# Reordering the steps of a neighbourhood-attention layer: earlier queries, projections and transposes behind the scores, bias tables spread over the opening

## The chip, the cores and the metric

The kernel runs on one core of a Trainium2 chip, in one launch. The metric is the device time of that launch in microseconds (us). Five engines of a core work side by side, each through its own instructions in order: PE (TensorE: matmuls and transposes, its weight loads listed as PEld), ACT (ScalarE), DVE (VectorE), POOL (GpSimd) and SP (SyncE, which here only issues DMAs). They wait for each other by semaphores.

## What is computed

Four layers over an image batch x of 4 x 56 x 56 x 128, all in fp32. The change concerns layer 0 alone, a neighbourhood attention with 4 heads of 32 channels, in which each pixel looks at the 7 x 7 pixels around it:

```python
qkv = (x @ w_qkv + b_qkv).reshape(B_, H_, W_, 3, nh, hd)
...
k_win = kk[:, :, idx_i][:, :, :, :, idx_j]
v_win = v[:, :, idx_i][:, :, :, :, idx_j]
...
attn = jnp.einsum('bnijd,bnipjqd->bnijpq', q, k_win) + bias[None]
attn = jax.nn.softmax(attn.reshape(B_, nh, H_, W_, k * k), axis=-1)
...
out = jnp.einsum('bnijpq,bnipjqd->bnijd', attn, v_win)
...
x = x + _L0_conv_ref(_gn(x), L0_conv_w_qkv, L0_conv_b_qkv, L0_conv_rpb, L0_conv_w_proj, L0_conv_b_proj)
```

`_gn` is a group norm over each image and group of 4 channels, and the last step of the layer is `out @ w_proj + b_proj`. Layer 1 is a selective scan, layer 2 a tanh attention and a mixture of experts, layer 3 an attention and a mixture of experts; their code is the same before and after.

## The kernel before

**Tiles.** The four images lie in SBUF for the whole program, as X[b]. In layer 0 (`layer0`, L354) an image is cut into NCH = 7 chunks of SEQ = 8 pixel rows, CH = 448 pixels. A chunk's keys are taken in bands of 8 columns; a band's window of 14 rows x 8 columns fills 112 partitions. The 7 bands are done in two groups, the even ones (four bands) and the odd ones (three), so a chunk gives two **units** and the four images give 28 chunks and 56 units. Even unit numbers are the groups of four.

**Steps.** For each chunk: `queries` (L438: one matmul group, then ACT writes q), `keys` (L447: the same into the one key buffer kT), `values` (L459: in two halves, each copied out by ACT). For each unit: `scores` (L481: PE writes two psum tiles "s" of two banks each), `weights` (L495: ACT takes exponentials, then DVE multiplies three heads and POOL one by a table of exponentiated biases), `sums` (L508: PE sums weights times values into psum "o", and the weights alone into "d"). After a chunk's second unit, `finish` (L526) has four steps: `copied` (L532: ACT copies d and o out of psum, POOL adds the projection's bias to X), `divided` twice (L539: DVE takes reciprocals of half the denominators and multiplies), `projected` (L544: PE multiplies by w_proj, DVE adds the result to X at L550).

**The next image's norm** runs beside an image. `norm_steps` (L401) has twelve steps: seven `chunk` steps, each with four transposes of X on PE (`turn`, L225), their statistics on DVE (`stats`, L235) and a copy of the raw transposes by ACT (`raw_bands`, L219); then the aggregate, two small matmuls that average over a group, with DVE steps after them and a square root on ACT; then the root with the normalisation of four chunks on DVE, and `hand_over` with the other three. In the last image `next_norm` (L424) does the same for layer 1, without the raw copies.

**Buffers.** Queries, keys, each half of the values, transposes, projections and the group matmuls all write to the psum tag "m", which has two buffers: each of these waits until the user of the buffer two allocations before is through. The tag "s" has two buffers, "o" and "d" one each; q, v and oT have two in SBUF.

**Order.** The program fixes the order on PE, ACT, DVE and POOL by hand (`manual_schedule`, L369); only waits are added. Before the loop come the bias tables: `bias_tables` (L301) loads its inputs, `spread` lays them out, and each of 24 `table` steps (L339) has four matmuls into an "s" buffer and one exponential on ACT. Eight are made at once, one after each of the seven chunk steps of the first image's norm, four during its group matmuls, five in the loop's first iteration. Image 0 is loaded from ACT's queue in four cuts ahead of the tables' inputs; all other loads come from SP's queue.

The loop (L601) is a plan: the dictionary `mid` holds steps that an iteration issues before its sums, `at` those that it issues after them:

```python
for i in range(len(units) + 5):
    if i + 1 < len(units):
        scores(i + 1)
        weights(i + 1)
    for step in mid.get(i, []):
        step()
    if 0 <= i - 1 < len(units):
        sums(i - 1)
    for step in at.get(i, []):
        step()
```

So iteration i issues the scores and weights of unit i+1 and the sums of unit i-1. `first[k]` is the first unit of chunk k (2k). The queries of chunk k+1 stand in `at` of iteration first[k], right before the iteration that issues their first scores. The keys of a chunk stand in `at` at a place given by its number, the values and the chunk steps of the norm in `mid`, the other norm steps and the four steps of `finish` in `at`. Some 50 small steps that prepare layer 1's weights (`next_weights`, L597; most on DVE) are spread over `at` too.

Of the kernel before, what the change touches and what calls it, by code (L numbers as in the profile page):

```python
# [18 lines left out]
B, HW, C = 4, 56, 128  # L19
# [3 lines left out]
NT = S // TP  # L23
TC = 4
CH = TC * TP
NCH = S // CH
SEQ = CH // HW
# [111 lines left out]
class Hybrid:  # L139
# [214 lines left out]
    def layer0(self, wp1):  # L354
# [3 lines left out]
        nc, a, tc = self.nc, self.a, self.tc  # L358
        ET = mybir.EngineType
        with ExitStack() as ctx:  # L360
# [6 lines left out]
            m = lambda: self.t(ps_m, [P, 512], "m")  # L367
            ctx.enter_context(
                tc.manual_schedule(engines={ET.PE, ET.Activation, ET.DVE, ET.Pool})  # L369
            )  # L370
            self.load_image(0, nc.scalar, (0, TC, 3 * TC, 5 * TC, NT))
            tables, spread, table = self.bias_tables(
                wp, wp, lambda: self.t(sm, [TP, NH, CH], "e", bufs=3).rearrange("p h n -> p (h n)"), m,
                lambda: self.t(ps_s, [P, 2, 512], "s")[:TP, 0],
            )
            group = self.load(wp, [P, P], "group", a["k_group"])
            wqkv = self.load(wp, [P, 3 * C], "wqkv", a["L0_conv_w_qkv"])
            bqkv = self.t(wp, [P, 3], "bqkv")
# [15 lines left out]
            chunks = [(b, c) for b in range(B) for c in range(NCH)]  # L394
            units = [(k, g) for k in range(len(chunks)) for g in range(len(PARTS))]
# [5 lines left out]
            def norm_steps(b):  # L401
                g = self.group_norm(b, big, group)

                def chunk(c):
                    if c == 0:
                        g.place_bands(big)
                    g.turn(c, m)
                    g.stats(c)
                    g.raw_bands(c)

                def hand_over():
                    g.normed(range(4, NCH))
                    xn[b] = g.xn

                parts = g.groups(m)
                both = lambda fs: lambda: [f() for f in fs]
                return (
                    [lambda c=c: chunk(c) for c in range(NCH)]
                    + [parts[0], both(parts[1:3]), both(parts[3:5])]
                    + [lambda: (parts[5](), g.normed(range(0, 4))), hand_over]  # L420
                )


            def next_norm():  # L424
                g = self.first_norm = self.group_norm(0, wp1, group)
                parts = g.groups(m)
                both = lambda fs: lambda: [f() for f in fs]
                chunk = lambda c: lambda: (g.turn(c, m), g.stats(c))
                return (
                    [chunk(c) for c in range(NCH)]  # L430
                    + [parts[0], both(parts[1:3]), both(parts[3:5]), parts[5]]
                )
# [40 lines left out]
            def parts(i):  # L473

                got, at = [], 0
                for band, j0, j1 in PARTS[units[i][1]]:
                    got.append((band, j0, j1, at))
                    at += j1 - j0
                return got

            def scores(i):  # L481
                k, g = units[i]
                t = top(chunks[k][1])
                sc[i] = [self.t(ps_s, [P, 2, 512], "s") for _ in range(2)]
                for band, j0, j1, at in parts(i):
                    for h in range(NH):
                        own = slice(h * HD, (h + 1) * HD)
                        to = sc[i][h // 2][:TP, h % 2, : SEQ * WIDTHS[g]]
                        nc.tensor.matmul(
                            by_row(to, WIDTHS[g])[:, :, at : at + j1 - j0],  # L490
                            kT[own, band, t : t + ROWS, :].rearrange("p r j -> p (r j)"),
                            by_row(q[k][own, :])[:, :, j0:j1], start=True, stop=True,
                        )

            def weights(i):  # L495
                k, g = units[i]
                c = chunks[k][1]
                n = SEQ * WIDTHS[g]
                es[i] = e = self.t(sm, [TP, NH, CH], "e", bufs=3)
                for j, s in enumerate(sc.pop(i)):  # L500
                    nc.scalar.activation(e[:, 2 * j : 2 * j + 2, :n], s[:TP, :, :n], AF.Exp)
                tab = tables[0 if c == 0 else 2 if c == NCH - 1 else 1]
                at = sum(WIDTHS[:g])
                for eng, h0, h1 in ((nc.vector, 0, 3), (nc.gpsimd, 3, NH)):
                    p = e[:, h0:h1, :n].rearrange("p h (q j) -> p h q j", j=WIDTHS[g])
                    eng.tensor_tensor(p, p, tab[:, h0:h1, :, at : at + WIDTHS[g]], op=ALU.mult)
# [19 lines left out]
            def finish(k):  # L526

                b, c = chunks[k]
                x = self.X[b][:, TC * c : TC * (c + 1), :]
                r = {}  # L530

                def copied():  # L532
                    r["o"], r["d"] = self.t(sm, [P, CH], "oT"), self.t(sm, [P, CH], "d", bufs=1)
                    ps = dict(zip("od", out.pop(k)))
                    for n in "do":
                        nc.scalar.copy(r[n], ps[n][:, :CH])
                    nc.gpsimd.tensor_add(x, x, bproj.unsqueeze(1).to_broadcast([TP, TC, C]))

                def divided(n):  # L539
                    own = slice(n * 2 * TP, (n + 1) * 2 * TP)  # L540
                    nc.vector.reciprocal(r["d"][:, own], r["d"][:, own])
                    nc.vector.tensor_mul(r["o"][:, own], r["o"][:, own], r["d"][:, own])

                def projected():  # L544
                    ps = m().rearrange("p (k c) -> p k c", c=C)
                    for i in range(TC):
                        nc.tensor.matmul(
                            ps[:TP, i, :], r["o"][:, i * TP : (i + 1) * TP], wproj, start=True, stop=True
                        )
                    nc.vector.tensor_add(x, ps[:TP], x)  # L550

                return [copied, lambda: divided(0), lambda: divided(1), projected]

            spread()
            for i in range(SEQ):
                table(0, i)
            rest = [(k, i) for k in (1, 2) for i in range(SEQ)]
            nc.vector.tensor_scalar(bq, bqkv[:, 0:1], HD**-0.5, None, op0=ALU.mult)
            for step, n in zip(norm_steps(0), [1] * NCH + [2, 2, 0, 0, 0]):
                step()  # L560
                for _ in range(n):
                    table(*rest.pop(0))
            nc.scalar.activation(bq_exp, bq, AF.Exp)
# [12 lines left out]
            first = {}  # L576
            for i, (k, _) in enumerate(units):
                first.setdefault(k, i)
            at, mid = {}, {}
            add = lambda i, f, *args, to=at: to.setdefault(i, []).append(lambda: f(*args))  # L580
            for k, i in rest:
                add(0, table, k, i, to=mid)
            for k, (b, c) in enumerate(chunks):
                i = first[k]
                end = first.get(k + 1, len(units))
                for n, step in zip((0, 0, 1, 3), finish(k)):
                    add(end + n, step)
                if k + 1 < len(chunks):
                    add(i, queries, k + 1)
                    for half in range(2):  # L590
                        add(i + half, values, k + 1, half, to=mid)
                if k >= 3:
                    add(first[k - 1] - 2 if c == 1 else first[k - 3] + (1 if c else 3), keys, k)
                if c == 0:
                    for n, step in enumerate(norm_steps(b + 1) if b + 1 < B else next_norm()):
                        add(i + n, step, to=mid if n < NCH else at)
            for n, step in enumerate(next_weights):  # L597
                add(first[2] + n * 50 // len(next_weights), step)
            scores(0)
# [1 line left out]
            for i in range(len(units) + 5):  # L601
                if i + 1 < len(units):
                    scores(i + 1)
                    weights(i + 1)
                for step in mid.get(i, []):
                    step()
                if 0 <= i - 1 < len(units):
# [3 lines that stand above are left out]
# [1539 lines left out]
```

## Time and profile before

| | |
|---|---|
| median of 3 runs | 7094.28 us (7087.53 to 7094.53) |
| the profiled execution | 7082.4 us |
| its span in the profile | 7080.6 us |
| of it layer 0, up to layer 1's first weight load on PE | 0 to 418.57 us |
| mean granted TensorE clock | 0.93 |
| busy in layer 0's part | PE 334.66, PEld 266.68, DVE 274.77, ACT 214.22, POOL 150.84 us |
| busy in the rest (6662.03 us) | PE 5731.51, PEld 2361.86, DVE 5493.64, ACT 4617.66, POOL 2726.41 us |

The profile is one execution. A group's line gives where an instruction is in the code, engine, operation, the tile written and those read, shapes, and busy time. A wait names the instruction that waited and the one that released it, then total us, how often, and the longest. In the timeline each row is: start and duration in us, engine, line, operation, tiles, count, and in brackets the engine's idle time before it and what ended it. Clock is the share of full speed granted to PE. A busy PE counts matmuls until their results are written, so back-to-back matmuls overlap; the step from one start to the next is the better price.

### The profile page before, as it was taken

How to read it: one execution, taken by the hardware profiler on the slowest of the kernel's cores; microseconds unless marked ns; L12 is line 12 of the kernel's file. 1: busy time of each engine (PE TensorE's matmuls, PEld its weight loads, DVE VectorE, ACT ScalarE, POOL GpSimd, SP SyncE). 2: the span in 40 equal slices, each digit the busy share in tenths (PEclk: the TensorE clock that was granted, in tenths of full speed). 3: DMA queues.
4: the chain of work that ended last, by engine and by line, in shares of the span. 5: the costliest groups of instructions: out<-in, count | busy, mean ns of one | idle time of the engine just before them, and what ended most of it. 6: DMA issues, size and time to landing. Idle time of an engine off the chain costs nothing.

```text
span 7080.6 us, 101476 instructions
## 1 busy us (share of the span) xinstructions
PE 6066.2 (86%) x37386; PEld 2628.5 (37%) x37386; DVE 5768.4 (81%) x10108; ACT 4831.9 (68%) x4827; POOL 2877.2 (41%) x1920
## 2 busy tenths in 40 slices
PE   7889999999999999977777867877778889999998
PEld 6642333333233333232223323332333355555554
DVE  5769999999999999978888888888888763566665
ACT  5557667776766677669998998999899833322231
POOL 3459989998999899921000001100101100000000
PEclk9989989999999899889999999999899999999999
DMA  2037767776776677700000000000003304243433
GB/s 51 6 89 187 184 168 177 188 182 171 187 185 176 168 188 185 186 14 3 1 3 6 8 1 6 6 6 3 6 3 114 106 10 148 74 111 93 112 89 93
DMA packets 363462, 654.19 MB, mean 92 GB/s; under 512 B 95428, under 2 KB 211924, under 8 KB 362453
## 3 DMA queue, kind: packets, MB, share of 16 engines
q1 hardware_dynamic: 359765, 646.10, 35.7%
q8 instruction: 295, 4.83, 0.3%
q10 hardware_dynamic: 3200, 1.61, 0.1%
q14 instruction: 202, 1.65, 0.1%
HBM read 536.78 MB, written 104.37 MB: 91 GB/s over the span
## 4 chain that ended last, share of the span: by engine, by line
PE 22%; ACT 12%; DVE 11%; issue 9%; POOL 1%; SPq 0%; DMA 0%; DVEq 0%; ACTq 0%; POOLq 0%
ACT th L1252 10%; PE o L1890 6%; DVE th L1243 6%; PE q L1878 5%; PE s L1266 4%; PE pe L2085 2%; DVE X L2090 2%; ACT e L1280 1%; POOL e L1287 1%; PE o L1296 1%; PE m L1424 1%; DVE wide L1910 1%; PE m L1199 1%; DVE X L1432 0%; PE m L1707 0%
## 5 line engine op out<-in xcount | busy, mean ns | idle before, releaser
L1252 ACT ACTIVATE th<-th 128x5488 f32<-128x5488 f32 (+13 forms) x560 | 2184.7, 3944 | 175.6 <-DVE th L1243 150.1
L1243 DVE TENSOR_SCALAR th<-fT,g 128x784 f32<-128x784 f32 (+13 forms) x3920 | 1869.1, 549 | 304.9 <-PE s L1266 286.8
L833 POOL TENSOR_TENSOR hs<-hs,bc 128x896 f32<-128x896 f32 x896 | 1856.3, 2091 | 119.3 <-DVE hs L828 115.6
L1266 PE MATMUL s<-th,place 128*32 128x392 f32 (+5 forms) x14112 | 1388.8, 488 | 444.9 <-ACT th L1252 442.1
L828 DVE TENSOR_TENSOR_SCAN hs<-E,u 128x896 f32<-128x896 f32 x728 | 1449.4, 2006 | 1.8 <-ACT E L812 1.8
L812 ACT ACTIVATE E<-E,rate 128x448 f32<-128x448 f32 x1456 | 885.9, 661 | 114.6 <-DMA E<-delta_dram 111.2
L1266 PEld LDWEIGHTS s<-th,place 128*32 128x32 f32 (+1 forms) x14112 | 454.5, 111 | 1313.1 <-ACT th L1252 669.2
L774 PE MATMUL u<-du,pick 32*128 32x448 f32 x2912 | 814.1, 627 | 142.5 <-DVE hs L828 139.2
L821 DVE TENSOR_TENSOR u<-u,bc 128x896 f32<-128x896 f32 x728 | 783.7, 1077 | 66.7 <-PE u L774 66.4
L1883 ACT ACTIVATE e<-q,shift 128x448 f32<-128x448 f32 (+1 forms) x511 | 321.9, 632 | 672.8 <-PE q L1878 650.9
L1287 POOL TENSOR_TENSOR e<-e,later 112x112 f32<-112x112 f32 x112 | 154.4, 1379 | 1133.6 <-ACT e L1280 680.3
L2090 DVE SCALAR_TENSOR_TENSOR X<-pe,r_gate,X 112x128 f32<-112x128 f32 x896 | 311.9, 348 | 308.5 <-PE pe L2085 272.6
L839 PE MATMUL y<-hs,sum 128*32 128x448 f32 x3584 | 498.8, 630 | 4.0 <-POOL hs L833 4.0
L1878 PE MATMUL q<-xT 128*128 128x448 f32 (+1 forms) x1022 | 500.8, 572 | 0.9 <-ACT e L1883 0.9
L1890 PE MATMUL o<-e,xk 128*128 128x448 f32 (+1 forms) x1022 | 478.8, 552 | 16.1 <-ACT oT L1855 16.1
L1296 PE MATMUL o<-e,xk 112*128 112x392 f32 (+5 forms) x1024 | 388.3, 499 | 91.4 <-POOL e L1287 87.7
L774 PEld LDWEIGHTS u<-du,pick 32*128 32x128 f32 x2912 | 245.3, 195 | 575.7 <-DVE hs L828 221.8
L1183 POOL MEMSET xa<- 112x4 f32 (+1 forms) x32 | 55.1, 1723 | 971.7 <-PE m L1176 971.7
L2019 POOL MEMSET lc_xa<- 112x4 f32 x28 | 3.1, 110 | 945.6 <-DVE lc_xa L2013 696.7
L821 POOL TENSOR_TENSOR V<-V,bc 128x896 f32<-128x896 f32 x168 | 350.3, 2085 | 13.0 <-DMA V<-du_dram 13.0
L816 ACT ACTIVATE u<-u 128x896 f32<-128x896 f32 x168 | 151.9, 904 | 296.5 <-PE u L765 216.9
L828 DVE TENSOR_TENSOR_SCAN hs<-u,V 128x896 f32<-128x896 f32 x168 | 338.2, 2013 | 0.0
(274 smaller groups left out, 7878.6 us busy)
## 6 DMA issues: line engine op xcount, KB each, us to landing
E<-delta_dram SPq DMA_DIRECT2D x728, 448.0 KB
V<-du_dram SPq DMA_DIRECT2D x168, 448.0 KB
wide<-in_L_ffn_weight SPq DMA_DIRECT2D x64, 1024.0 KB
r<-M SPq DMA_DIRECT2D x189, 224.0 KB
M<-wide SPq DMA_DIRECT2D x72, 392.0 KB
du_dram<-du SPq DMA_DIRECT2D x224, 112.0 KB
delta_dram<-delta SPq DMA_DIRECT2D x224, 112.0 KB
M<-wide SPq DMA_DIRECT2D x72, 168.0 KB
```

The source lines that it names most:

```text
L774: nc.tensor.matmul(halves(to)[:, k], w["pick"][own, q, :], pre[j]["du"][own, f], start=True, stop=True,)
L812: nc.scalar.activation(e, e, AF.Exp, scale=rate)
L821: eng.tensor_mul(v, v, pre[p // PAIRS]["bc"][:, 0:1].to_broadcast([P, 2, CH]))
L828: nc.vector.tensor_tensor_scan(flat, E.pop(p), V.pop(p), 0.0, op0=ALU.mult, op1=ALU.add)
L833: nc.gpsimd.tensor_mul(HS[p], HS[p], bc[:, 1:2].to_broadcast([P, 2, CH]))
L839: nc.tensor.matmul(py[j, f][r * HD : (r + 1) * HD, :], w["sum"][:, q, :], HS[p + r // 2][:, r % 2], start=False, stop=(q == QG - 1),)
L1243: nc.vector.tensor_scalar(th[i][:, s, lo:hi], fT[j][:, lo:hi], g[b, J // WT][:, at : at + 1], None, op0=ALU.add,)
L1252: nc.scalar.activation(own, own, AF.Tanh)
L1266: nc.tensor.matmul(ps[j, J][QW * blk : QW * blk + rows, h, lo:hi], place[:, off : off + rows], z[:, at + s, h * HALF + lo : h * HALF + hi] ...
L1296: nc.tensor.matmul(po[j][:, h, lo:hi], xk[b, J // WT][:, J % WT, :], e[:, h * HALF + lo : h * HALF + hi], start=(J == 0), stop=(J == t + ( ...
L1878: nc.tensor.matmul(ps[:n, :CH], of_tile(xT[b], t), xT[b][:, c * CH : (c + 1) * CH], start=True, stop=True,)
L1890: nc.tensor.matmul(po[b, c], xk[b][:n, t, :], e[:n], start=first, stop=last)
```

## The change

Nothing is computed differently; the instructions of layer 0 are issued in another order, and image 0 is loaded from another queue.

- **Loads.** Image 0 goes from ACT's queue to SP's: its first cut (four of 28 row pairs, one chunk) before the tables' inputs, the rest in two cuts behind them instead of three.
- **Tables.** Two tables come before the first image's norm instead of eight. One still follows each chunk step and four the group matmuls; then four follow the root and two follow `hand_over`. Five stay in the loop's first iteration.
- **Queries** of chunk k+1 are issued one iteration earlier (first[k]-1). Where several steps fall into one iteration's `at`, the norm steps now come first and keys are put in before queries.
- **A new place**, between an iteration's scores and its weights, takes the steps `early` (the projection of a finished chunk, with its add on DVE) and `turns` (the norm's chunk steps: transposes and statistics). `raw_bands` is handed back as a function and is issued right behind the weights. Before, the projection stood in `at`, and the whole chunk step in `mid`, beside the halves of the values.

```diff
@@ -368,11 +368,12 @@
             ctx.enter_context(
                 tc.manual_schedule(engines={ET.PE, ET.Activation, ET.DVE, ET.Pool})
             )
-            self.load_image(0, nc.scalar, (0, TC, 3 * TC, 5 * TC, NT))
+            self.load_image(0, cuts=(0, TC))
             tables, spread, table = self.bias_tables(
                 wp, wp, lambda: self.t(sm, [TP, NH, CH], "e", bufs=3).rearrange("p h n -> p (h n)"), m,
                 lambda: self.t(ps_s, [P, 2, 512], "s")[:TP, 0],
             )
+            self.load_image(0, cuts=(TC, 4 * TC, NT))
             group = self.load(wp, [P, P], "group", a["k_group"])
             wqkv = self.load(wp, [P, 3 * C], "wqkv", a["L0_conv_w_qkv"])
             bqkv = self.t(wp, [P, 3], "bqkv")
@@ -406,7 +407,7 @@
                         g.place_bands(big)
                     g.turn(c, m)
                     g.stats(c)
-                    g.raw_bands(c)
+                    return lambda: g.raw_bands(c)
 
                 def hand_over():
                     g.normed(range(4, NCH))
@@ -425,7 +426,9 @@
                 g = self.first_norm = self.group_norm(0, wp1, group)
                 parts = g.groups(m)
                 both = lambda fs: lambda: [f() for f in fs]
-                chunk = lambda c: lambda: (g.turn(c, m), g.stats(c))
+                def chunk(c):
+                    return lambda: (g.turn(c, m), g.stats(c)) and None
+
                 return (
                     [chunk(c) for c in range(NCH)]
                     + [parts[0], both(parts[1:3]), both(parts[3:5]), parts[5]]
@@ -551,13 +554,18 @@
 
                 return [copied, lambda: divided(0), lambda: divided(1), projected]
 
+            def run(step):
+                rest_of_it = step()
+                if callable(rest_of_it):
+                    rest_of_it()
+
             spread()
-            for i in range(SEQ):
-                table(0, i)
-            rest = [(k, i) for k in (1, 2) for i in range(SEQ)]
+            rest = [(k, i) for k in range(3) for i in range(SEQ)]
             nc.vector.tensor_scalar(bq, bqkv[:, 0:1], HD**-0.5, None, op0=ALU.mult)
-            for step, n in zip(norm_steps(0), [1] * NCH + [2, 2, 0, 0, 0]):
-                step()
+            table(*rest.pop(0))
+            table(*rest.pop(0))
+            for step, n in zip(norm_steps(0), [1] * NCH + [2, 2, 0, 4, 2]):
+                run(step)
                 for _ in range(n):
                     table(*rest.pop(0))
             nc.scalar.activation(bq_exp, bq, AF.Exp)
@@ -576,24 +584,25 @@
             first = {}
             for i, (k, _) in enumerate(units):
                 first.setdefault(k, i)
-            at, mid = {}, {}
+            at, mid, early, turns = {}, {}, {}, {}
             add = lambda i, f, *args, to=at: to.setdefault(i, []).append(lambda: f(*args))
             for k, i in rest:
                 add(0, table, k, i, to=mid)
             for k, (b, c) in enumerate(chunks):
+                if c == 0:
+                    for n, step in enumerate(norm_steps(b + 1) if b + 1 < B else next_norm()):
+                        add(first[k] + n, step, to=turns if n < NCH else at)
+            for k, (b, c) in enumerate(chunks):
                 i = first[k]
                 end = first.get(k + 1, len(units))
-                for n, step in zip((0, 0, 1, 3), finish(k)):
-                    add(end + n, step)
+                for n, to, step in zip((0, 0, 1, 3), (at, at, at, early), finish(k)):
+                    add(end + n, step, to=to)
+                if k >= 3:
+                    add(first[k - 1] - 2 if c == 1 else first[k - 3] + (1 if c else 3), keys, k)
                 if k + 1 < len(chunks):
-                    add(i, queries, k + 1)
+                    add(max(i - 1, 0), queries, k + 1)
                     for half in range(2):
                         add(i + half, values, k + 1, half, to=mid)
-                if k >= 3:
-                    add(first[k - 1] - 2 if c == 1 else first[k - 3] + (1 if c else 3), keys, k)
-                if c == 0:
-                    for n, step in enumerate(norm_steps(b + 1) if b + 1 < B else next_norm()):
-                        add(i + n, step, to=mid if n < NCH else at)
             for n, step in enumerate(next_weights):
                 add(first[2] + n * 50 // len(next_weights), step)
             scores(0)
@@ -601,7 +610,11 @@
             for i in range(len(units) + 5):
                 if i + 1 < len(units):
                     scores(i + 1)
+                then = [step() for step in early.get(i, []) + turns.get(i, [])]
+                if i + 1 < len(units):
                     weights(i + 1)
+                for step in then:
+                    run(lambda: step)
                 for step in mid.get(i, []):
                     step()
                 if 0 <= i - 1 < len(units):
```

## The prediction

> **What bounds the kernel now.** I first cut the trace by stage. Layer 0 fills the first 418.57 us of the 7080.6 us span, and the diff touches nothing later, so only these 418.57 us are at stake. Iteration i of its main loop issues the scores of unit i+1, then the sums of unit i-1; an image has 14. The windows below, cut where a unit's scores start on PE, are one opening window, the three kinds of stretch in an image, and the tail (columns: window and length, then busy us of PE, PEld, DVE, ACT, POOL, then clock).
>
> ```profile
> 0.00:38.37 38.37, 28.58 (x210) 24.79 (x210) 11.75 (x36) 21.92 (x37) 1.47 (x7) 0.96 0.74 130
> ...
> 108.20:137.96 29.76, 22.66 (x392) 17.28 (x391) 22.85 (x31) 13.42 (x22) 9.78 (x7) 0.89 0.01 2
> 137.96:187.39 49.43, 38.92 (x693) 30.65 (x692) 31.38 (x39) 25.62 (x44) 20.09 (x12) 0.93 0.02 7
> 187.39:203.13 15.74, 14.76 (x308) 12.06 (x308) 12.48 (x18) 9.70 (x15) 7.41 (x4) 1.00 0.01 3
> ...
> 330.40:372.56 42.16, 36.41 (x693) 27.96 (x692) 31.46 (x38) 22.55 (x37) 20.11 (x12) 1.00 0.01 2
> ...
> 388.31:418.57 30.26, 21.19 (x404) 17.69 (x404) 24.67 (x29) 10.55 (x18) 8.56 (x8) 0.87 0.01 2
> ```
>
> PE is busiest (38.92 of 49.43) but idles 10.5 us in seven iterations that also transpose the next image ("turn iterations"). Its waits from 40 to 417 us say for what:
>
> ```profile
> PE s L489 <- ACT q L445: 22.0, 24, 1.6
> PE m L464 <- DVE X L550: 15.6, 3, 5.3
> PE m L440 <- ACT xnT L220: 10.9, 9, 1.2
> PE m L547 <- ACT xnT L220: 7.0, 5, 1.7
> ```
>
> The first is queries issued just ahead of the scores that need them. The second comes three times, where one image hands over to the next. The others are the two buffers "m" held by a raw copy (L220). The timeline shows the chain behind those:
>
> ```profile
> 72.36 0.60 PE L228 MATMUL m<-ident,X 112*128 112x112 f32 x4
> ...
> 73.98 1.21 DVE L506 TENSOR_TENSOR e<-e,tab 112x1008 f32<-112x1008 f32 x1 [2.10 <-ACT e L501]
> ...
> 75.11 0.63 DVE L238 BATCH_NORM_STATS2 gn_st<-m 128x6 f32<-128x448 f32 x1
> 75.77 0.53 ACT L220 COPY xnT<-m 128x448 f32<-128x448 f32 x1 [1.89 <-DVE gn_st L238]
> ...
> 76.35 1.02 PE L440 MATMUL m<-xnT,wqkv 128*128 128x448 f32 x2 [1.20 <-ACT xnT L220]
> ...
> 77.52 0.67 ACT L445 ACTIVATE q<-m,bq 128x448 f32<-128x448 f32 x1
> ...
> 78.24 1.09 PE L489 MATMUL s<-q,kT 32*112 32x104 f32 x32 [0.87 <-ACT q L445]
> ```
>
> The transposes end at 72.96, yet their statistics stand behind DVE's multiply until 75.11; so the copy, the queries, q and the next scores are all late: 2.07 us of PE idle in this one iteration.
>
> **What the Trainium skill says.** "TensorE: Matmul & The Clock Gate", Part 1, What's actually happening: PE falls to half clock after an idle window of about 3.4 us and needs about as long busy to return. The trace agrees: the handover window has clock 0.89, that is 29.76 x 0.11 x 2 = 6.5 us at half rate behind a 5 us stall; the opening matmuls start 0.187 us apart until 11.2 us and 0.098 after. "PSUM — Partial Sum Buffer", PSUM bank collisions raise a hardware error: two engines may not be in one bank at once, reads included; this is why a raw copy waits for the statistics (75.11 + 0.63, then 75.77). "SBUF — State Buffer", Who interferes with whom: a DVE op with two SBUF inputs contends with a GpSimd read. Agrees: POOL's 112x448 multiply took 2.45 beside DVE's and 1.12 at 116.74. "DMA: Bandwidth & Descriptors", Issuing engines are not separate DMA queues: loads share 16 engines whoever issues them; so image 0 gains no bandwidth by leaving ACT.
>
> **The change, part by part.** PE prices are start-to-start steps of the timeline at full clock: scores 1.03 (even unit) or 0.78 (odd), transposes 0.34, values 1.06 or 0.84, sums 1.30 or 1.70, projection 0.86, keys 0.95, queries 0.95.
>
> *Turn pairs.* New order in an even iteration: odd scores 0.78, transposes 0.34, values 1.06, sums 1.30 = 3.48. Odd iteration: even scores 1.03, projection 0.86, transposes 0.34, values 0.84, sums 1.70, queries 0.95, keys 0.95 = 6.67. The pair is 10.15 if nothing waits. Queries now have an iteration of 3.48 us over q's 0.65 on ACT: that wait is gone (q has two buffers; the older was last read two iterations before). The statistics run at 1.48 to 2.10 while ACT computes exponentials (0.95 to 2.30), so the raw copy is clear at 2.83. What is late next: the second values reuse the "m" that the projection filled, freed by DVE's X add (L550), and that add is now queued on DVE behind the first reciprocal. The denominator copy starts after the sums end (3.48), ends at 4.16; reciprocal 1.55, multiply 0.39, a layer-1 weight step about 0.35: DVE is free at 6.5, adds to 7.2. PE reaches the values at 5.71, so it waits about 1.5 us; statistics and the weight multiply queue behind that add, but their sums come an iteration later. A turn pair is 3.48 + 8.2 = 11.7. The unshown cost is this wait: from 0 (projection landing in DVE's gap) to 3 (POOL in DVE's way on top); I take 1.5. Seven turn iterations are 4 x 3.48 + 3 x 8.2 = 38.6.
>
> *Three iterations after them.* Without transposes the pair is 9.5 (0.68 less, no wait: values reuse a buffer freed by a copy). But these are odd, even, odd, and now both queries and keys sit in odd ones: 6.3 + 3.4 + 6.6 = 16.3 with the group-norm matmuls and a wait on an add behind the mean's small ops.
>
> *Handover (four iterations).* DVE has 22.85 us of work in 29.76, and the diff removes none. Root and four normalisations (about 5 us), then a division (1.9), now stand ahead of an X add that frees the buffer for the next image's queries; I work out an add at 13.0 against PE ready at 7.6, again a stall over 5 us, again half clock. PE then does queries, keys, scores, values in about 13 us at full rate, some 2 more at half: 28.3. The gain is 1 to 2 of 30.
>
> *Opening.* Image 0 moves to SP's queue: its first cut is issued first and sets rpb, same, cols, kill back by one issue (0.44); the other two set group and all later loads, image 1 and layer 1's included, back by up to 1.3 us in all. Image 1 is needed after 40 us and by the bytes of the DMA view was through about 18, so that is covered; uncovered it would cost the same 1.3. ACT no longer issues: its table load stood at 6.82 behind four issues. Two tables instead of eight run ahead of the transposes. At half rate (8 x 0.187 = 1.5 each) from about 5.6 they, one transpose step and one table take PE to 10.9; then six steps of 1.16 put the last transposes at 16.7, where they were at 22.16: 5.5 earlier. The six tables return behind the root: PE idles 3.67 us there now, but two psum buffers and an Exp table reload (1.28) let only two start; queries come about 7.7 after the variance matmul instead of 3.7, 4.0 later. Net 1.5, and 1.5 for a half-rate stretch (the keys) that the filled gap avoids: 3.0. Bounds: 0 and 7.
>
> *Sum*, now to new: opening -3.0; 38.37 to 53.17, -0.5. Image 0: turn 39.27 to 30.9 (no projections in its first four iterations), after 15.76 to 16.3, handover 29.76 to 28.3. Image 1: 49.43 to 38.6, 15.74 to 16.3, 30.17 to 28.3. Image 2: 50.77 to 38.6, 17.30 to 16.3, 29.03 to 28.3. Image 3: 42.16 to 38.6, 15.75 to 16.3, tail 30.26 to 29.3 (DVE's reciprocals end it). Together -43. Layer 1 follows in order on every engine, so all of it arrives. The profiled execution took 7082.4 us and would take 7039; the median shown, 7094.28, is 12 higher, so 7051.
>
> **Rivals.** *PE-bound throughout*: the X add never delays PE and the clock never halves. the 12 turn pairs with a projection save 1.5 more each (18), handovers 3 x 2, opening 4 more: -71, 7023. Against: 9.4 us of DVE work in a pair of 10.15. *A wash*: the add behind the reciprocal costs 3 to 4 us a pair and non-turn pairs gain nothing: 1.5 to 2.5 us x 14 lost from 43 leaves -8 to -22; about 7080, near the line of 0.2%. For: image 3's pairs, without a raw copy, are 12.06 today, so DVE's order matters. *Slower*: the new stall of PE before the second values trips the clock gate in each turn pair. Two half-rate windows of 3.4 us cost up to 3.4 us a pair: 14 x 3.4 = 48, and one more in each handover, 3 x 3.4 = 10: 7094 - 43 + 58 = 7109. It decides if the stall alone passes 3 us; against it, pairs that idle 1.37 of 12.06 now keep clock 1.00. *It doesn't do what it says*: queries do move a full iteration; I see no room for this.
>
> **Chances.** 0.2% is 14 us, about what a measurement of this kernel tells from no change. Forecast (-20 to -66) 0.68; PE-bound 0.10; wash 0.15, a third of it past -14; slower 0.07. Faster 0.83, same 0.10, slower 0.07. Low end: just past the PE-bound 7023. High end: the forecast with the 3 us stall (+21) and no gain in opening or handovers (+8), -14, rounded to 7083.
>
> **What would show it.** Right: "s L489 <- ACT q" nearly gone; statistics straight behind the transposes; a new wait of values (L464) on X L550 in turn pairs, about 1.5 us each; turn stretches near 38.6; a handover stall of about 5 us, now at queries (L440). Wrong: turn stretches above 45, clock below 0.9 in them, or queries(0) no earlier than 31.22.

## The result, and the profile after

The changed kernel takes 7039.76 us (median of 6 runs, 7028.64 to 7047.55) against 7090.84 us for the kernel before (6 runs, 7083.58 to 7094.53). The ratio is 0.993, 95% interval 0.9917 to 0.9942: 0.6 to 0.8% faster, some 51 us where 43 were forecast. The profiled execution took 7044.67 us, its span is 7042.9.

In this profile layer 0 ends at 373.85 us instead of 418.57: 44.7 us earlier. The rest of the program, whose instructions are the same, took 6669.05 against 6662.03 us. Over the ten profiles of this study that rest lies between 6657.7 and 6669.0 with no relation to the edit, so those 7 us are not the change's. I therefore read small effects from the length of layer 0 and its stretches, and use the run times to see that they arrive.

Line numbers have moved: scores are L492 (before L489), values L467 (L464), keys L453 (L450), queries L443 (L440), projection L550 (L547), X add L553 (L550), reciprocals L544 (L541), the scaling of the query bias L564 (L558).

The windows of the changed kernel, cut at the same units as before (window, length, busy us of PE, PEld, DVE, ACT, POOL, clock):

```profile
0.00:41.65 41.65, 31.48 (x209) 28.18 (x209) 11.55 (x36) 21.74 (x37) 1.46 (x7) 0.88 0.70 123
...
100.28:127.62 27.34, 22.72 (x391) 17.00 (x390) 22.81 (x34) 14.10 (x23) 9.75 (x6) 0.88 0.01 2
127.62:166.10 38.48, 34.31 (x692) 27.92 (x691) 28.29 (x36) 23.53 (x40) 13.83 (x10) 1.00 0.03 9
...
346.28:373.85 27.57, 19.49 (x403) 17.03 (x403) 23.58 (x30) 10.74 (x18) 9.06 (x7) 0.88 0.01 2
```

The turn stretch of the second image went from 49.43 to 38.48 us and PE's idle time in it from 10.5 to 4.2, at full clock throughout. In the kernel before, the granted clock halves twice in that stretch, for 3.41 us each; so up to 3.4 of the 11.0 us gained are clock. The opening grew from 38.37 to 41.65. The waits of PE from 40 to 375 us (what waited, for what, total us, times, longest):

```profile
PE m L467 <- DVE X L553: 13.9, 10, 1.5
PE m L453 <- DVE X L553: 8.9, 3, 3.1
PE m L550 <- DVE oT L545: 7.2, 3, 3.8
...
PE s L492 <- ACT q L448: 0.7, 1, 0.7
...
PE m L443 <- ACT xnT L220: 0.2, 1, 0.2
```

The wait of scores on q fell from 22.0 to 0.7 us, those of queries and projections on the raw copies (L220) from 10.9 + 7.0 to 0.2. A new one leads the list: values on the X add, 13.9 us in ten waits of up to 1.5. One such place in the timeline of the changed kernel:

```profile
131.12 1.09 PE L492 MATMUL s<-q,kT 32*112 32x104 f32 x32
...
132.14 1.13 PE L550 MATMUL m<-wproj,oT 128*112 128x128 f32 x8
132.17 1.55 DVE L544 RECIPROCAL d<-d 128x224 f32<-128x224 f32 x1 [0.94 <-ACT d L539]
...
133.10 0.55 PE L228 MATMUL m<-ident,X 112*128 112x112 f32 x4
133.83 0.39 DVE L545 TENSOR_TENSOR oT<-oT,d 128x224 f32<-128x224 f32 x1
134.14 0.28 DVE L708 TENSOR_SCALAR D_diag<-ident,D 128x128 f32<-128x128 f32 x1
...
134.34 0.68 DVE L553 TENSOR_TENSOR X<-m,X 112x512 f32<-112x512 f32 x1
...
135.07 0.91 PE L467 MATMUL m<-wqkv,xnT 128*112 128x128 f32 x6 [1.42 <-DVE X L553]
```

The projection's matmuls end at 133.27, but its X add stands on DVE behind a reciprocal, a multiply and a weight step until 134.34; the values need the buffer that it frees and start 1.42 us late. Everything else on PE follows without a gap.

The handover still stalls, now at the keys. The first one:

```profile
109.16 0.99 PE L443 MATMUL m<-xnT,wqkv 128*128 128x448 f32 x2 [0.61 <-DVE xnT L285]
...
112.22 0.68 DVE L553 TENSOR_TENSOR X<-m,X 112x512 f32<-112x512 f32 x1
...
112.96 1.86 PE L453 MATMUL m<-xnT,wqkv 128*128 128x448 f32 x2 [2.81 <-DVE X L553]
```

The queries wait 0.61 us for a normalisation, then the keys 2.81 us for an X add.

The opening in the timeline of the changed kernel (the rows SPq are SP issuing a load):

```profile
4.20 2.51 SPq L164 DMA_DIRECT2D group<-in_k_group  x1
...
7.24 0.43 SPq L381 DMA_DIRECT2D bqkv<-in_L_conv_b_qkv  x1
...
12.79 0.15 DVE L564 TENSOR_SCALAR bq<-bqkv 128x1 f32<-128x1 f32 x1 [7.56 <-DMA bqkv<-in_L_conv_b_qkv]
12.86 1.15 DVE L238 BATCH_NORM_STATS2 gn_st<-m 128x6 f32<-128x448 f32 x2
13.52 0.53 ACT L220 COPY xnT<-m 128x448 f32<-128x448 f32 x1 [4.82 <-DVE gn_st L238]
...
14.11 0.60 PE L228 MATMUL m<-ident,X 112*128 112x112 f32 x4 [3.26 <-ACT xnT L220]
```

The same load and the same instruction in the kernel before:

```profile
4.37 0.43 SPq L380 DMA_DIRECT2D bqkv<-in_L_conv_b_qkv  x1
...
9.23 0.15 DVE L558 TENSOR_SCALAR bq<-bqkv 128x1 f32<-128x1 f32 x1 [4.07 <-DMA bqkv<-in_L_conv_b_qkv]
```

The first statistics stand on DVE behind the scaling of the query bias (L564), and that waits for a load of 1.5 KB until 12.79 us, where it began at 9.23 before. The raw copies wait for the statistics, and PE's third transposes wait 3.26 us for a buffer.

### The profile page after: what moved, and what is told of

The parts are those of the page before. It is cut to its first block, busy times and chain, and to the rows that moved or that the text cites. A ratio compares the mean times of both kernels' runs of the same rounds, so it can differ in the third digit from the quotient of the medians.

```text
span 7042.9 us, 101461 instructions
## 1 busy us (share of the span) xinstructions
PE 6058.3 (86%) x37386; PEld 2624.0 (37%) x37386; DVE 5762.5 (82%) x10108; ACT 4833.4 (69%) x4827; POOL 2853.0 (41%) x1920
## 4 chain that ended last, share of the span: by engine, by line
PE 22%; ACT 12%; DVE 11%; issue 8%; POOL 1%; SPq 0%; DMA 0%; DVEq 0%; ACTq 0%; POOLq 0%
ACT th L1265 10%; PE o L1903 6%; DVE th L1256 6%; PE q L1891 5%; PE s L1279 4%; DVE X L2103 2%; PE pe L2098 2%; ACT e L1293 1%; POOL e L1300 1%; PE o L1309 1%; PE m L1437 1%; DVE wide L1923 1%; PE m L1212 1%; DVE X L1445 0%; PE m L1720 0%
## 5 line engine op out<-in xcount | busy, mean ns | idle before, releaser
L1903 PE MATMUL o<-e,xk 128*128 128x448 f32 (+1 forms) x1022 | 479.5, 553 | 16.7 <-ACT oT L1868 16.7
```

What stands on the lines that cost most here:

```text
L1903: nc.tensor.matmul(po[b, c], xk[b][:n, t, :], e[:n], start=first, stop=last)
```

## The experiments

The first four kernels stand between the kernel before and the changed one; the last four are the changed kernel with one edit each, e8 with three. All stretches are read from the profiles: where the scores of a unit start on PE, in us. "Turn" is the seven turn iterations of the second to the fourth image, "after" the three iterations behind them (mean of four images), "handover" four iterations (mean of three). "Turn" holds four even and three odd iterations, "after" one even and two odd. The earlier queries move work from an even into an odd iteration, so kernels with and without them are better compared by a pair of iterations than by either column.

| kernel | first scores | turn (images 2, 3, 4) | after | handover | layer 0 ends | ratio to before (95%) |
|---|---|---|---|---|---|---|
| before | 38.37 | 49.4, 50.8, 42.2 | 16.1 | 29.7 | 418.57 | 1 |
| changed | 41.65 | 38.5, 38.4, 38.8 | 15.9 | 27.5 | 373.85 | 0.993 (0.9917, 0.9942) |
| e1_queries | 37.98 | 47.0, 44.8, 37.2 | 18.4 | 29.6 | 411.48 | 0.9983 (0.9975, 0.9992) |
| e2_places | 37.70 | 41.6, 41.6, 41.7 | 15.7 | 27.2 | 380.37 | 0.9949 (0.9934, 0.9964) |
| e3_loop | 38.55 | 38.5, 38.4, 38.8 | 15.9 | 27.6 | 373.47 | 0.9933 (0.9918, 0.9947) |
| e4_opening | 43.37 | 49.1, 49.4, 42.2 | 16.1 | 29.6 | 422.03 | 0.9997 (0.9989, 1.0006) |
| e5_bias_late | 37.47 | 38.5, 38.4, 38.8 | 15.9 | 27.3 | 369.46 | 0.992 (0.9905, 0.9935) |
| e6_division | 39.98 | 35.7, 35.7, 35.7 | 15.6 | 27.6 | 362.54 | 0.9911 (0.9894, 0.9927) |
| e7_norm_spread | 41.96 | 38.5, 38.4, 38.8 | 15.9 | 24.2 | 364.58 | 0.9922 (0.9907, 0.9937) |
| e8_all_three | 34.39 | 36.1, 36.0, 36.0 | 15.8 | 25.3 | 356.33 | 0.9905 (0.989, 0.992) |

The medians of e5, e6 and e7 (7029.64, 7025.19 and 7033.00 us) lie below the changed kernel's, but their intervals overlap its interval: the size of each gain rests on one profile.

**e1_queries: the queries alone.**

```diff
-                    add(i, queries, k + 1)
+                    add(max(i - 1, 0), queries, k + 1)
```

> The kernel before with one edit: the queries of a chunk are issued one iteration earlier. Opening, projection and transposes stay where they were. Theory (the gains overlap, since one PE chain has several late ends): the wait of scores on q goes, but projection, queries and keys then wait for the psum buffers that the raw copies hold behind DVE's multiply, so a turn pair falls from 14.2 to about 12 us and a pair without transposes from 10.4 to 9.5; together about -30 us, ratio 0.996. Rival (the gains are separate and add up): only the 22 us of waits on q in the list of waits go, ratio 0.997, and the waits on the raw copies stay at about 20 us.

Measured: layer 0 is 7.1 us shorter. Both expectations were too high, mine by more. Its waits of PE:

```profile
PE m L547 <- ACT xnT L220: 14.3, 5, 3.6
...
PE s L489 <- ACT q L445: 0.7, 1, 0.7
```

The scores wait for q no more, but the projection now waits 14.3 us for buffers that the raw copies hold (7.0 before), and all waits on raw copies come to 21.9 us (19.6 before): these stayed, as the rival said. Projection, queries and keys, three users of the two buffers, now stand in a row in one iteration; that this is why is argued, not tested. A pair without transposes takes 11.1 us in the first image against 10.9, so most of the 18.4 against 16.1 in the table is the cut of the windows. Removing the longest wait of the list bought a third of its 22 us.

**e2_places: projection and chunk steps behind the scores, alone.** The changed kernel with the opening of before (the edit shown at e3) and the queries where they were. It also has the new order of the steps within `at`, whose share is not measured apart:

```diff
-                    add(max(i - 1, 0), queries, k + 1)
+                    add(i, queries, k + 1)
```

> The kernel before with one edit: projection and chunk steps go between scores and weights, the raw copy behind the weights. Queries and opening stay. Theory (overlap): in turn pairs the slip from q (about 0.9 us) is hidden in the stall that the second values have anyway until DVE's X add, so turn stretches are near 39 us as with the whole change; pairs without transposes stay near 10.4. Together about -38 us, ratio 0.9945. Rival (add up): the waits on q stay in full, turn stretches stay near 43, about -27 us, ratio 0.996.

Measured: layer 0 is 38.2 us shorter. The size is the theory's, the way to it only half: turn stretches of 41.6 lie between the two expectations, and the waits on q stayed as the rival said:

```profile
PE s L491 <- ACT q L447: 24.6, 24, 1.6
...
PE m L466 <- DVE X L552: 4.7, 10, 0.5
```

The wait of the values on the X add shrank to 0.5: PE comes later to it. So in a turn pair the slip from q mostly fills that stall (12.0 us a pair against 11.7 in the changed kernel), while a pair without transposes pays it (10.9 against 9.6).

**e3_loop: both, with the opening of before.**

```diff
-            self.load_image(0, cuts=(0, TC))
+            self.load_image(0, nc.scalar, (0, TC, 3 * TC, 5 * TC, NT))
...
-            self.load_image(0, cuts=(TC, 4 * TC, NT))
...
-            table(*rest.pop(0))
-            table(*rest.pop(0))
-            for step, n in zip(norm_steps(0), [1] * NCH + [2, 2, 0, 4, 2]):
+            for i in range(SEQ):
+                table(0, i)
+            rest = [(k, i) for k in (1, 2) for i in range(SEQ)]
+            for step, n in zip(norm_steps(0), [1] * NCH + [2, 2, 0, 0, 0]):
```

> The whole change of the loop (queries, projection, transposes, raw copies) with the opening of the kernel before. Theory: the new opening costs time, because DVE's scaling of the query bias waits for a small load that now queues behind image 0; with the old opening the first scores start at 38.4 instead of 41.65 and the run is about 3 us faster than with the whole change: -50 us, ratio 0.993. Rival: the later first scores of the profile are an accident of the clock gate, and the old opening gives nothing or loses: -42 us, ratio 0.994.

Measured: layer 0 is 45.1 us shorter than before, the sum of e1 and e2 (7.1 + 38.2 = 45.3). That the totals agree is in part chance: in the turn and after stretches of the first two images both parts together gain 6.8 us more than their sum, and elsewhere as much less. So neither the overlap that I had supposed nor a plain sum describes it. The first scores start at 38.55, 3.1 us before the changed kernel's; the loop's first iterations, 1.4 us longer, and other small differences give most of that back, so layer 0 gains only 0.4. The run times do not part this kernel from the changed one.

**e4_opening: the new opening alone.** The reverse of e3's edit, in the kernel before.

> The kernel before with the new opening alone: image 0 on SP's queue, two tables instead of eight ahead of the transposes, six more behind the root. Theory: first scores about 3 us later than 38.4, the first statistics on DVE behind the bias scaling at about 12.8 us, PE waiting about 3 us for the first raw copy; ratio 1.000 to 1.0005. Rival: without the loop's change the opening gains the 3 us that the prediction had for it, first scores at about 35.4, ratio 0.9995.

Measured: the first scores at 43.37, 5.0 us later, and layer 0 3.5 us longer; the ratio can't tell it from no change. PE's wait of transposes on the raw copy is there, 3.1 us. So the new opening delays the first scores with the old loop (5.0) as with the new (3.1), but of that 3.5 and 0.4 us reach the end of layer 0 in the profiles, and no run time shows it.

**e5_bias_late: the bias scaling moved behind the norm.**

```diff
-            nc.vector.tensor_scalar(bq, bqkv[:, 0:1], HD**-0.5, None, op0=ALU.mult)
             table(*rest.pop(0))
...
+            nc.vector.tensor_scalar(bq, bqkv[:, 0:1], HD**-0.5, None, op0=ALU.mult)
             nc.scalar.activation(bq_exp, bq, AF.Exp)
```

> The changed kernel with one DVE instruction moved: the scaling of the query bias is issued behind the first image's norm instead of ahead of it; loads and tables stay. Theory (the opening lost because the statistics queue behind this instruction, which waits for a load behind image 0): the first statistics start near 9 us instead of 12.9, PE's 3.3 us wait at the third transposes goes, and with it the half-rate stretch behind it; first scores at about 36.7 instead of 41.65, ratio to the kernel before 0.9926. Rival (the opening lost because six tables moved behind the root and image 0 lands later): the first scores stay at 40 or later and the time stays that of the changed kernel.

Measured: first scores at 37.47, layer 0 4.4 us shorter than the changed kernel's. Its timeline has the statistics where the transposes end:

```profile
8.86 0.63 DVE L238 BATCH_NORM_STATS2 gn_st<-m 128x6 f32<-128x448 f32 x1 [3.63 <-PE m L228]
...
9.53 0.53 ACT L220 COPY xnT<-m 128x448 f32<-128x448 f32 x1 [0.82 <-DVE gn_st L238]
```

PE's wait at the third transposes is gone, and the last transposes end at 17.06 us instead of 21.11. One instruction of 0.15 us ahead of its load was the opening's loss. In the four kernels with the new opening it starts at 12.46 to 14.21 us, in the four with the old one at 9.03 to 10.23. PE's later wait of 2.30 us before the tables is still there, and so is a half-rate stretch of 6.83 us; without it the first scores come at 34.39 (e8).

**e6_division: the X add ahead of both divisions.**

```diff
-                for n, to, step in zip((0, 0, 1, 3), (at, at, at, early), finish(k)):
+                for n, to, step in zip((0, 1, 1, 3), (at, at, at, early), finish(k)):
```

> The changed kernel with one step moved: the first division of a chunk is issued one iteration later, beside the second, so that DVE's X add of a projection stands ahead of both. Theory (the second values wait because that add queues behind the first reciprocal): the waits of L467 on the X add fall from 1.4 us to about 0.5 each, a turn pair from 11.7 to about 10.7, the handover by about 2 us as the first queries' buffer is freed earlier; first-to-last about -16 us beyond the changed kernel, ratio 0.991. Rival (DVE as a whole is the bound of a turn pair, 9.4 us of work and what POOL takes from it): the wait only moves to another instruction and the turn pair stays within 0.3 us of 11.7.

Measured: turn stretches 35.7 instead of 38.5, layer 0 11.3 us shorter. Of these, 1.7 are in the opening, which the edit doesn't touch.

```profile
PE m L443 <- DVE X L553: 8.4, 3, 3.3
...
PE s L492 <- ACT kT L457: 7.0, 3, 3.0
PE m L467 <- DVE X L553: 4.7, 10, 0.5
```

The waits of the values fell from 13.9 to 4.7 us, 0.5 each, as worked out, and a turn pair takes 10.7 us; DVE is not the bound of a pair of 11.7. The handover did not move (27.6), against the expectation: PE waits as long there, now at the queries and, 3.0 us at most, for the keys that follow them.

**e7_norm_spread: the seven normalisations spread.**

```diff
                 def hand_over():
-                    g.normed(range(4, NCH))
+                    g.normed((2,))
                     xn[b] = g.xn
+                later = [lambda: None, lambda: g.normed((3,))]
+                for c in range(4, NCH):
+                    later += [lambda: None, lambda c=c: g.normed((c,))]
...
-                    + [lambda: (parts[5](), g.normed(range(0, 4))), hand_over]
+                    + [lambda: (parts[5](), g.normed((0, 1)) and None), hand_over] + later
...
```

> The changed kernel with the seven normalisations of a new image spread: two behind the root, one with the handover, the other four one by one in the four odd iterations after it, instead of four and three at once. Theory (the handover is DVE's backlog ahead of the X add): the wait of queries or keys on the X add falls by about 1.3 us per image and the handover from 27.5 to about 25.5 us; the normalisations that move into turn pairs lengthen those by up to 0.3 each; net about -4 us, ratio 0.9925. Rival (the handover is the clock at half rate and PE's own work): 27.5 stays and the turn pairs grow, net +2 us.

Measured: handovers of 24.2 us instead of 27.5, turn stretches as before the edit, layer 0 9.3 us shorter. The second handover in its windows and the turn stretch behind it:

```profile
179.41:203.67 24.26, 20.34 (x392) 15.47 (x391) 22.38 (x31) 14.09 (x23) 7.81 (x6) 1.00 0.01 2
203.67:242.06 38.39, 34.30 (x691) 27.91 (x690) 31.42 (x40) 23.60 (x40) 13.70 (x10) 1.00 0.03 9
```

The wait of the keys is shorter by 0.9 us (2.2 at most, 3.1 in the changed kernel), the handover by 3.3. The rest goes with the clock, 1.00 where it was 0.88: 27.34 x 0.12 x 2 = 6.6 us at half rate are gone, worth up to 3.3. That the shorter wait is what spared the clock is not shown, and e8 speaks against it.

**e8_all_three.** The edits of e5, e6 and e7 together.

> The changed kernel with all three edits: the bias scaling behind the norm, the first division beside the second, the normalisations spread. If each theory holds: first scores at about 36.7, turn pairs about 10.8, handovers about 24, layer 0 about 345 us instead of 374, ratio to the kernel before 0.989. If DVE bounds the turn pairs: only the opening's 5 us are left beyond the changed kernel, ratio 0.9925.

Measured: ratio 0.9905 (0.989 to 0.992) to the kernel before, median 7018.62 us: the fastest of all; against the changed kernel the medians differ by 21 us, while the two intervals (to before) just touch. Layer 0 ends at 356.33, not at 345, and the edits alone add up to 4.4 + 11.3 + 9.3 = 25.0 where 17.5 came. Two places show where. Its first turn stretch (six iterations) is 33.6 us against 29.5 in e6, with a wait of PE that names no other instruction and a half-rate stretch of 3.4 us behind it; its handovers are 25.3, not 24.2, at clock 0.93, with the waits for the keys of e6:

```profile
PE s L496 <- ACT kT L461: 5.6, 3, 2.3
...
PE o L526 <- issue: 2.8, 1, 2.8
```

("Issue" is time for which the profile shows no cause.) What makes that wait stays open. In the second handover no wait of PE is longer than 1.8 us, and the clock fell all the same; in e7 it stayed at 1.00 with waits of up to 2.2.

## Why the prediction was right, and where it was not

| term of the sum | predicted | measured |
|---|---|---|
| opening | -3.0 | +3.3 |
| 38.37 to 53.17 | -0.5 | -2.1 |
| turn stretches, images 1 to 4 | -8.4, -10.8, -12.2, -3.6 | -9.2, -11.0, -12.4, -3.4 |
| three iterations after | +0.5, +0.6, -1.0, +0.6 | +0.1, 0.0, -1.2, +0.2 |
| handovers | -1.5, -1.9, -0.7 | -2.4, -2.6, -1.4 |
| tail | -1.0 | -2.7 |
| layer 0 | -43 | -44.7 |

**The total: right, in part by luck.** The opening missed by 6.3 us, and the other terms together gained 8 more than worked out; hence -44.7 against -43.

**Turn pairs: right in mechanism and size.** Worked out 11.7 us and 38.6 for seven iterations; measured 11.5 to 11.8 (3.50 and 8.00 to 8.30) and 38.4 to 38.8. The stall where it was expected, about 1.5, measured 1.2 to 1.5, and e6 shows its cause by taking most of it away. The statistics behind the transposes and the end of the waits on q are in the waits above; e2 and e1 put 38 us to the places and 7 to the queries, which had led the list of waits with 22.

**Handovers and tail: right in kind, somewhat too small a gain.** The stall remained, and so did a clock of 0.88. I had the stall at the queries, over 5 us; it came at the keys (L453), 2.8 to 3.1, with 0.6 at the queries ahead of them. The X add itself ended where I had it, 12.6 us into the first handover against 13.0; but PE was ready at 8.3, not 7.6, and did the queries first: they waited for a normalisation and not for that buffer, so they had the other one. That DVE's backlog ahead of the add sets the stall, e7 shows in part: with normalisations moved away it is 0.9 us shorter.

**The opening: wrong, in sign.** The first step that failed is "set group and all later loads, image 1 and layer 1's included, back by up to 1.3 us in all", which I took as covered. I named image 1 as what could wait and passed over the query bias, a load of 1.5 KB between them, which one DVE instruction awaits ahead of the first statistics. SP issued that load 2.9 us later, at 7.24 instead of 4.37, as the issue of group's load alone took 2.51 us; it was usable at 12.79 instead of 9.23. Before, eight tables ran until 15.2 and hid that instruction; the change took the cover away.

Four profiles with the old opening have first scores at 37.70 to 38.55 (mean 38.2), four with the new one at 39.98 to 43.37 (mean 41.7): +3.6. With the instruction moved (e5, e8) they are at 37.47 and 34.39: 4 to 7 us sooner, so the new opening, rid of this, does gain, 0.7 (e5) and 3.8 (e8) against the old openings; 3.0 was worked out. The transposes then come as worked out: the last ones start at 16.51 and 16.17, forecast 16.7.

What parts e5 from e8 is the second step that failed, "1.5 for a half-rate stretch (the keys) that the filled gap avoids": the gap shrank from 3.67 to 2.30 us, but a half-rate stretch of 3.41 or 6.83 us still stands there in all kernels with the new opening but e8.

**The rivals.** PE-bound throughout: no, 13.9 us of waits on the X add and half rate in every handover. A wash: no, the stall is 1.4 and not 3 to 4. Slower, by the clock gate in each turn pair: no, clock 1.00 in all turn stretches with that stall. These rivals counted 12 and 14 pairs; the trace has ten such waits, three in each of the last three images as in the forecast's own 4 x 3.48 + 3 x 8.2, and one in the first. The high end is a slip as well: 7094 - 14 is 7080, not 7083.

**The run time.** It came out 11 us below the 7051 forecast. Of these, 3.4 are the median before, 7094.28 from three runs then and 7090.84 from six now, and 1.7 are layer 0; the other 6 are not traced to anything. The profile came out 5 us above the forecast for it (7082.4 - 43), since the rest of the program was 7.0 us longer there; that rest varies by 11 us from profile to profile.

## What to carry to other kernels

With an order set by hand, follow each released buffer to the instruction that frees it and then along that engine's queue: here the same two buffers moved from raw copies to an add behind a reciprocal, and one place further in e6, and the length of the next stall in a turn pair could be worked out from row durations to 0.3 us. In the handover the time of the add came out as well, but the stall was 2 us off, because I had the wrong one of two buffers waiting. When cover is taken away at the start of a program, list every instruction that was behind it and the load that each awaits, the smallest too. The longest wait of a list is not what its removal brings: queries alone gave 7 of their 22 us.

## What the runs showed of the hardware that I had not expected

The start differs from profile to profile by more than most edits change it: with nearly the same opening code the first scores came at 39.98, 41.65, 41.96 and 43.37 us. The load of the query bias was usable at 12.46 to 14.21 us in these four, and the half-rate stretches stand at different times (from 15.7 and 29.4 in the changed kernel, from 14.0 and 31.0 in e4_opening).

The length of a wait does not decide whether the clock halves. The prediction took an idle window of about 3.4 us for it; but in the kernel before it halved in the second image's turn stretch with no wait of PE above 1.75 us, and not in the first image's, with waits as long. Every half-rate stretch in layer 0 of the ten profiles lasts 3.41 or 6.83 us. At one and the same wait of 2.3 us, before the tables in the opening, there is one of 6.83 us in the changed kernel, e4 and e5, one of 3.41 in e6 and e7, and none in e8. The same matmuls of e5 and of e8:

```profile
25.75 6.27 PE L344 MATMUL s<-cols,e 112*112 112x98 f32 x32 [2.30 <-ACT tab L348]
```

```profile
25.42 3.52 PE L344 MATMUL s<-cols,e 112*112 112x98 f32 x32 [2.30 <-ACT tab L348]
```

So a single profile can gain or lose up to 3.4 us at such a place without the edit; what decides stays open.
